# A two-layer graph attention kernel for 32 graphs: the first graph's projection taken head by head, masks of the first and last graph by transfer, W1's place used again

## The chip, the cores and the metric

The kernel runs on one core of one Trainium2 chip. The metric is the time of one execution in device microseconds (us), lower is better. Everything computed is float32. Engines are named as in the profile: PE does matrix products and PE transposes, PEld is its weight load, DVE and ACT do elementwise work, POOL issues accumulating transfers and computes one small power, SP issues all other transfers.

## The reference

For each of 32 graphs (`x` is 32 x 512 x 512, `adj` 32 x 512 x 512) the reference normalises the nodes, runs two graph attention layers and adds the result to `x`:

```python
h = relu(layernorm(x))
mask = (adj > 0) | eye(512)
h = elu(gat_layer(h, mask, W1, att_src1, att_dst1, b1, concat=True))    # H=4 heads of F=256
x = x + gat_layer(h, mask, W2, att_src2, att_dst2, b2, concat=False)    # 1 head of 512

def gat_layer(x, mask, W, a_src, a_dst, bias, concat):
    xl = (x @ W).reshape(B, N, H, F)
    asrc, adst = einsum('bnhf,hf->bnh', xl, a_src), einsum('bnhf,hf->bnh', xl, a_dst)
    e = leaky_relu(asrc[:, :, None, :] + adst[:, None, :, :], 0.2)
    attn = softmax(where(mask[..., None], e, -1e9), axis=1)
    out = einsum('bsdh,bshf->bdhf', attn, xl)
    return (out.reshape(B, N, H * F) if concat else out.mean(axis=2)) + bias
```

## The kernel before

**Work per graph.** A graph's 512 nodes are four tiles of 128 partitions. `load` brings them, `norm` computes mean and variance on DVE and the power -1/2 on POOL (one call for all four tiles), `norm_turn` scales them on ACT and turns them into `ht` (features on partitions). For the first graph the turn is made of PE transposes, for all others of a DMA transpose with two ACT passes around it. `project1` makes `xl`, four heads of 256 columns and, in two further columns of W1, the scores. `Soft.first` finds each head's softmax minimum and sum, `Soft.second` makes its weights `p` (one scalar_tensor_tensor on DVE per tile, then the mask, then an exponential on ACT), `gather1` multiplies `p` with `xl` and an ELU gives `h1`. `project2`, a second `Soft` and `gather2` do the same for layer 2, and `residual` loads `x` again with the bias added.

**Products.** Most products are taken by seven half-size products instead of eight (`sevens`, `gather1`), whose sums DVE makes ahead and whose results ACT copies (four of seven) or DVE adds (three of seven). Three are plain: the first graph's projection (`project1_first`, in the order head pair, node tile, head; all copies on ACT), and `gather1_plain` for the first graph and, through `PLAIN = 1`, for the second.

**Masks.** `masks` turns `adj` into `m`, in SBUF, keeps a copy in DRAM (`dm`) and a transposed one (`mt`). In `second` the mask is added to `p` by two accumulating transfers from `dm` on POOL's queue, except where `here` is true: three of four heads of the first graph's layer 1, and all of the last graph (four heads and layer 2). There DVE adds `m` tile by tile.

**Places.** `p` has three slots, each a whole head's weights. `w1_sb` holds W1 in seven blocks; once the last graph is projected, a part of it holds layer 2's `xl` of the last graph but one.

**Order.** `Program` records every operation with a cost and its dependences. PE's order is the order in which the program was written. The order on ACT, DVE, POOL and SP comes from a planner: rounds of list scheduling, forwards and backwards, and then 40 times a step `sooner`, which raises the rank of what TensorE waited for, over the whole program; the order with the earliest modelled end is emitted. Each engine then runs its own list in order, so an instruction that waits holds up all that stand behind it on that engine.

Of the kernel before, what the change touches and what calls it, by code (L numbers as in the profile page):

```python
# [44 lines left out]
class Program:  # L45
# [70 lines left out]
    def sooner(self, rank, start, cause):  # L116


        jobs, lost, free = self.jobs, {}, 0.0
        for j in range(len(jobs)):  # L120
            if jobs[j][0] != "PE":
                continue
            gap, free = start[j] - free, start[j] + jobs[j][1]
            d = cause[j]
            while gap > 0.05 and d is not None and start[j] - start[d] < self.SPAN:
                lost[d] = max(lost.get(d, 0.0), gap)
                d = cause[d]
        return [r - self.GAIN * lost.get(j, 0.0) for j, r in enumerate(rank)]

    SPAN, GAIN = 60.0, 2.0  # L130
# [60 lines left out]
    def order(self):  # L191
        jobs = self.jobs
        n = len(jobs)
        self.after = [[] for _ in range(n)]
        for j, job in enumerate(jobs):
            for d in job[2]:
                self.after[d].append(j)

        need, pe = [0.0] * n, None
        for j in reversed(range(n)):  # L200
            later = self.DMA_LEAD + self.DMA_TAIL + (jobs[j][4] or 0.0)
            need[j] = max(
                (
                    need[s] + jobs[s][1] + (later if jobs[j][4] is not None else self.latency(j, s))
                    for s in self.after[j]
                ),
                default=0.0,
            )
            if jobs[j][0] == "PE":
                if pe is not None:  # L210
                    need[j] = max(need[j], need[pe] + jobs[pe][1])
                pe = j
        best, self.tried = None, []

        def look(rank):
            nonlocal best
            start, done, cause = self.forwards(rank)
            end = max(start[j] + jobs[j][1] for j in range(n))
            self.tried.append(end)
            if best is None or end < best[0]:  # L220
                best = end, start, done, cause, rank
            return start, cause

        rank = need
        for _ in range(self.ROUNDS):
            back = self.backwards(rank)
            rank = [-back[j] - jobs[j][1] for j in range(n)]
            start, cause = look(rank)
            rank = [-start[j] - jobs[j][1] for j in range(n)]
        _, start, _, cause, rank = best  # L230
        for _ in range(self.REPAIRS):
            rank = self.sooner(rank, start, cause)
            start, cause = look(rank)
        _, self.start, done, _, self.late = best
        return done

    REPAIRS = 40
# [7 lines left out]
def tile_gat(  # L245
# [101 lines left out]

    prog = Program()
# [27 lines left out]
    def w1_keys(ix):  # L376
        return [("w1", ix, k) for k in range(KQ)] + [
            ("w1s", ix, k, j) for k in range(KQ) for j in range(H // 2)
        ]
# [9 lines left out]
    def weights1():  # L389
        for c in range(2):  # L390
            for r in range(2):
                for k in range(KQ):
                    row = (r * KQ + k) * P
                    ix = AT[r, c]
                    dma(
                        0.75, (), [("w1", ix, k)], w1_sb[:, ix, k, :, 2:],
                        w1[row : row + P, :].rearrange("p (j c f) -> p c j f", j=H // 2, c=2)[:, c],
                    )

    def scores1():  # L400
# [8 lines left out]
        for j in range(H // 2):  # L409
            for c in range(2):  # L410
                for a in range(2):
                    for r in range(2):
                        for k in range(KQ):
# [3 lines left out]
                                0.4, [vk + ("v", a, j), ("w1", ix, k)], [("w1s", ix, k, j), jk],  # L417
# [11 lines left out]
    def weights2():  # L429
# [11 lines left out]
        for a, v in enumerate((as2, ad2)):  # L441
            lk, bc = ls.take()
# [12 lines left out]
            ls.give(lk)  # L455
# [20 lines left out]
    def masks(b):  # L476
# [15 lines left out]
        if b < B - 1:  # L492
            MASK[b] = mk, md = mds.take()
            dma(0.45, every, [mk], md.rearrange("p t n -> p (t n)"), m.rearrange("p t n -> p (t n)"))
# [10 lines left out]
    def norm(b):  # L505
        sk, st = stats.take()
        S, A = nc.vector.BN_STATS_DIM, nc.vector.BN_AGGR_DIM
        for t, (xk, xt) in enumerate(XT[b]):
            dve(0.61, [xk], [sk + (t,)], nc.vector.bn_stats, st[:, t, :S], xt)
            dve(TINY, [sk + (t,)], [sk + (t,)], nc.vector.bn_aggr, st[:, t, S : S + A], st[:, t, :S])  # L510
        every = [sk + (t,) for t in range(NT)]
        rstd = st[:, :, S + A]
        dve(TINY, every, every, nc.vector.tensor_scalar_add, rstd, st[:, :, S + 1], EPS)
        prog.add(
            "POOL", 1.0, every, every,
            lambda: nc.gpsimd.tensor_tensor(rstd, rstd, half, op=OP.pow),
        )
        shift = st[:, :, S]
        dve(
            TINY, every, every, nc.vector.scalar_tensor_tensor,  # L520
            shift, shift, -1.0, rstd, op0=OP.mult, op1=OP.mult,
        )
        ST[b] = sk, st

    def norm_turn(b, t):
# [7 lines left out]
        if b == 0:  # L533
# [37 lines left out]

    HERE = ()
# [5 lines left out]
    class Soft:  # L578
# [96 lines left out]
        def second(self, h):  # L675
# [3 lines left out]
            pk, p = ps_.take()  # L679

            here = self.b == B - 1 or self.layer == 1 and (h in HERE or self.b == 0 and h < H - 1)
# [150 lines left out]
    def project1_first(zt):  # L832

        for j in range(H // 2):
            zk, z = zt[j]
            for t in range(NT):
                for c in range(2):
# [5 lines left out]
                           for q in (("w1", AT[r, c], k), ("w1s", AT[r, c], k, j))],  # L843
# [9 lines left out]
                    act(COPY, [bk], keys, to, bt[:, 2:W], AF.Copy, scale=-1.0)  # L853
                    dve(TINY, [bk], [zk + (0, c, t)], nc.vector.tensor_copy, z[:, 0:2, c, t], bt[:, 0:2])
                    banks.give(bk)
                yield
# [52 lines left out]
    def sums1(h, pk, p):  # L909
# [41 lines left out]
    PAIR = (  # L951
        (0, 1), (1, 1), (0, 2), (1, 2), (0, 6), (1, 6), (0, 5), (1, 5), (0, 7), (1, 7), (0, 3), (1, 3),
        (0, 4), (1, 4),
    )

    def gather1(soft, j):

        blocks, bank = {}, {}
        for i in range(2):
            blocks[i] = sums1(2 * j + i, *soft.p[2 * j + i])  # L960
        for i, n in PAIR:
            left, right, late = blocks[i]
# [4 lines left out]
            if first:  # L967
                bank[i, acc] = banks.take()
            bk, bt = bank[i, acc]
# [11 lines left out]
            g = (2 * j + i) * FPH + r  # L981
# [12 lines left out]
        for i in range(2):  # L994
            ps_.give(soft.p.pop(2 * j + i)[0])
# [51 lines left out]
    def residual(b, places=(ts_,) * NT):  # L1047

        XR[b] = []
        for d in range(NT):  # L1050
# [6 lines left out]
            dma(0.75, (), halves, xr, x[b, d * P : (d + 1) * P, :])  # L1057
# [55 lines left out]
    def gather2_plain(b, soft):  # L1113
# [17 lines left out]
        ps_.give(pk)  # L1131
# [13 lines left out]
    PLAIN = 1  # L1145
# [5 lines left out]
    norm(0)  # L1151
    for t in range(NT):
        norm_turn(0, t)
    scores1()
    masks(0)
    given = [zs.take() for _ in range(2)]
    run(project1_first(given))
# [43 lines left out]
    for i in range(B - 1):  # L1201
# [3 lines left out]
        if i < PLAIN:  # L1205
            run(gather1_plain(s, (0, 1)))
        else:
            gather1(s, 0)
        s.second(2)
        s.second(3)  # L1210
        S2[i] = second_layer(i)
        if not last:
# [11 lines left out]
        if i < PLAIN:  # L1224
            run(gather1_plain(s, (2, 3)))
        else:
            gather1(s, 1)
        if last:
            S2[i].second(0)
# [14 lines left out]
        if last:  # L1244
# [3 lines left out]
            for _ in range(4):  # L1248
# [46 lines left out]
```

## Time and profile before

| what | value |
|---|---|
| time, median of 11 runs (lowest, highest) | 2814.37 us (2806.67, 2822.99) |
| the profiled execution: time, its span | 2815.55 us, 2813.7 us |
| PE busy | 2760.0 us, 98% |
| DVE busy | 2640.7 us, 94% |
| ACT busy | 2306.9 us, 82% |
| DMA engines, mean rate | 176 GB/s |
| accumulating transfers `p<-dm` on POOL | 304, median 5.2 us from issue to landing |

The span runs from the first instruction to the last; the time of an execution has a little more around it. Busy shares are means over the whole span. PE's busy time holds stretches at a lower granted clock too, so an idle PE and a slow PE both have to be looked for. A releaser named behind an idle time is the event that came last.

### The profile page before, as it was taken

What the parts mean: (1) busy time and instruction counts of PE and PEld (TensorE: products, weight loads), DVE (VectorE), ACT (ScalarE), POOL (GpSimd) and SP (SyncE); (2) the same over time, 40 slices, a digit from 0 to 9 for tenths busy, and PEclk for the clock granted to TensorE, in tenths of its full rate; (3) what the DMA queues carried; (4) which work ended last, traced back from release to release, by engine and by line L of the source; (5) the groups of instructions that cost most, each with busy time, mean ns of one, the idle gap of its engine ahead of it and who ended that gap; (6) DMA issues with size and microseconds to landing.
All of it is one profiled execution on the core that took longest, in us unless ns stands there. A gap on an engine that the chain in (4) does not pass through costs nothing.

```text
span 2813.7 us, 41284 instructions
## 1 busy us (share of the span) xinstructions
PE 2760.0 (98%) x12456; PEld 2371.0 (84%) x12456; DVE 2640.7 (94%) x6691; ACT 2306.9 (82%) x4861; POOL 311.5 (11%) x342
## 2 busy tenths in 40 slices
PE   6999999999999999999999999999999999999988
PEld 5668888788888888888888888888888788888876
DVE  6979999899999999999999999999999899999996
ACT  6878898788888888888888888888887788888872
POOL 0011111101111011111011101011101111110100
PEclk9999999999999999999999999999999999999999
DMA  7566776667776667766676766676766767666622
GB/s 219 137 157 176 188 195 168 167 175 192 184 199 169 179 178 197 186 176 176 183 190 179 200 168 181 175 204 170 200 177 170 170 175 200 174 177 167 184 72 98
DMA packets 371600, 494.73 MB, mean 176 GB/s; under 512 B 225200, under 2 KB 229296, under 8 KB 371376
## 3 DMA queue, kind: packets, MB, share of 16 engines
q1 hardware_dynamic: 327600, 332.68, 42.3%
q0 software_dynamic: 43776, 159.40, 23.9%
q8 instruction: 100, 1.64, 0.2%
q14 instruction: 124, 1.02, 0.1%
HBM read 312.22 MB, written 50.79 MB: 129 GB/s over the span
## 4 chain that ended last, share of the span: by engine, by line
PE 48%; DVE 4%; DMA 3%; ACT 2%; issue 1%; DVEq 0%; ACTq 0%; POOLq 0%
PE mm L368 48%; DMA p<-dm 1%; DVE p L354 1%; DMA x<-adj 1%; DVE h L354 1%; ACT l L351 0%; DVE l L354 0%; DVE t L354 0%; DMA mt<-m 0%; ACT p L351 0%; DVE hs L354 0%; ACT adj L351 0%; DVE xl L354 0%; DMA t<-in_x_dram 0%; ACT ht L351 0%
## 5 line engine op out<-in xcount | busy, mean ns | idle before, releaser
L368 PE MATMUL mm<-w_sb,hs 128*128 128x257 f32 (+1 forms) x3024 | 693.9, 384 | 18.6 <-DVE hs L354 11.1
L368 PEld LDWEIGHTS mm<-w_sb,hs 128*128 128x128 f32 x3024 | 578.8, 192 | 108.4 <-DVE hs L354 12.4
L362 POOL DMA_DIRECT2D p<-dm x304 | 267.4, 889 | 2379.1 <-DVE p L354 1579.8
L351 ACT ACTIVATE l<-as,z 128x512 f32<-128x512 f32 x640 | 444.2, 721 | 93.2 <-DMA as<-das 92.5
L351 ACT ACTIVATE l<-l,low 128x512 f32<-128x512 f32 x640 | 459.0, 720 | 49.4 <-DVE low L354 47.1
L368 PE MATMUL mm<-p,xl 128*128 128x256 f32 (+1 forms) x2016 | 489.2, 391 | 9.1 <-ACT p L351 4.6
L368 PE MATMUL mm<-w_sb,ht 128*128 128x258 f32 x2112 | 483.2, 383 | 6.3 <-DVE xl L354 4.0
L351 ACT ACTIVATE p<-p,z 128x512 f32<-128x512 f32 x640 | 432.0, 719 | 49.0 <-DMA p<-dm 27.4
L368 PE MATMUL mm<-w_sb,h 128*128 128x257 f32 x2056 | 467.8, 379 | 0.0
L368 PEld LDWEIGHTS mm<-w_sb,ht 128*128 128x128 f32 x2112 | 402.4, 191 | 67.9 <-DVE xl L354 5.7
L354 DVE SCALAR_TENSOR_TENSOR p<-rr,z 128x512 f32<-128x512 f32 x640 | 453.0, 742 | 5.2 <-DMA rr<-drr 4.9
L368 PEld LDWEIGHTS mm<-p,xl 128*128 128x128 f32 x2016 | 383.2, 191 | 85.2 <-issue 20.2
L354 DVE CUSTOM_DVE_ANT_1 l<-l,mt 128x512 f32<-128x512 f32 x640 | 427.4, 681 | 19.2 <-ACT l L351 16.1
L368 PEld LDWEIGHTS mm<-w_sb,h 128*128 128x128 f32 x2056 | 389.7, 190 | 57.5 <-issue 0.5
L351 ACT ACTIVATE xl<-mm 128x258 f32<-128x258 f32 (+2 forms) x752 | 280.9, 381 | 64.2 <-PE mm L368 62.2
L351 ACT ACTIVATE h<-mm 128x256 f32<-128x256 f32 x480 | 175.3, 379 | 112.8 <-PE mm L368 109.8
L354 DVE TENSOR_TENSOR xl<-xl,mm 128x258 f32<-128x258 f32 x558 | 221.6, 416 | 35.4 <-PE mm L368 30.6
L351 ACT ACTIVATE xr<-h,b_sb 128x512 f32<-128x512 f32 x240 | 169.5, 721 | 73.3 <-DVE h L354 57.6
L368 PE MATMUL mm<-t,hs 128*128 128x256 f32 x960 | 219.3, 382 | 0.3 <-ACT h L351 0.3
L368 PEld LDWEIGHTS mm<-t,hs 128*128 128x128 f32 x960 | 183.1, 191 | 26.7 <-ACT h L351 1.0
L354 DVE TENSOR_TENSOR t<-mm,t 128x256 f32<-128x256 f32 (+1 forms) x424 | 170.6, 414 | 15.4 <-PE mm L368 14.8
L368 PE MATMUL mm<-xl,p 128*128 128x256 f32 (+1 forms) x752 | 181.0, 390 | 4.0 <-ACT p L351 4.0
(105 smaller groups left out, 3374.5 us busy)
## 6 DMA issues: line engine op xcount, KB each, us to landing
p<-dm POOLq DMA_DIRECT2D x304, 512.0 KB, 5.2
rr<-drr SPq DMA_DIRECT2D x160, 512.0 KB
x<-in_x_dram SPq DMA_DIRECT2D x129, 256.0 KB
adj<-in_adj_dram SPq DMA_DIRECT2D x128, 256.0 KB
as<-das SPq DMA_DIRECT2D x64, 512.0 KB
t<-in_x_dram SPq DMA_DIRECT2D x124, 256.0 KB
out_dram<-t SPq DMA_DIRECT2D x124, 256.0 KB
dm<-m SPq DMA_DIRECT2D x31, 512.0 KB
```

The costliest lines, as they stand in the source:

```text
L351: prog.add("ACT", cost, reads, writes, lambda: nc.scalar.activation(*a, **k))
L354: prog.add("DVE", cost, reads, writes, lambda: f(*a, **k))
L362: lambda: nc.gpsimd.dma_start(to, at, accum_op=OP.add), size,
L368: f(*a, **k)
```

## The change

The diff is cut; "..." marks what is left out. It does these things:

- W1 is loaded in 16 pieces of 128 rows by one head, head by head, where it was 8 pieces of two heads. The first graph's norm is done for each tile of 128 nodes by itself (four power calls on POOL instead of one). Its projection starts with head 0 of the tiles that are turned, between the turns, and takes heads 0 and 1 over all tiles first, then heads 2 and 3 tile by tile. The copies of every second head move from ACT to DVE.
- The second graph is turned by PE transposes too (`b < 2`), and its `gather1` is by seven products (`PLAIN = 0`).
- Masks are added by transfer everywhere but in layer 2 of the last graph. The last graph's mask is therefore kept in DRAM too.
- Heads 2 and 3 of the last graph have their `p` in two places within W1's block (`pzs`), free once that graph is projected. The last graph's four heads are gathered in one order (`SINGLY`) that runs through all of them, with `second(2)`, `second(3)` and the previous graph's layer 2 started between.
- The residual's load waits for the first tile of layer 2's projection of that graph. The vectors of layer 2's scores use a slot of `t` instead of `l`. Two instead of four products of the last graph but two's `gather2` stand ahead of the last `project2`.
- The planner's repair works through the program in stretches of 80 PE operations, tries six settings of reach and weight in each, and keeps an order when it starts the PE operation 40 behind the stretch earlier. The whole order on ACT, DVE, POOL and SP is made anew by it.

```diff
...
-    def sooner(self, rank, start, cause):
+    def sooner(self, rank, start, cause, span, gain, first, last):
...
-            while gap > 0.05 and d is not None and start[j] - start[d] < self.SPAN:
+            while gap > 0.05 and d is not None and start[j] - start[d] < span:
                 lost[d] = max(lost.get(d, 0.0), gap)
                 d = cause[d]
-        return [r - self.GAIN * lost.get(j, 0.0) for j, r in enumerate(rank)]
-
-    SPAN, GAIN = 60.0, 2.0
+        return [r - gain * lost.get(j, 0.0) for j, r in enumerate(rank)]
+
+    WAYS = tuple((span, gain) for span in (60.0, 25.0) for gain in (2.0, 0.7, 6.0))
+    STRETCH = 80
...
-        _, start, _, cause, rank = best
-        for _ in range(self.REPAIRS):
-            rank = self.sooner(rank, start, cause)
-            start, cause = look(rank)
-        _, self.start, done, _, self.late = best
+
+        _, start, done, cause, rank = best
+        n_pe = len(self.tensor)
+        for first in range(0, n_pe, self.STRETCH):
+            last = min(first + self.STRETCH, n_pe)
+            goal = self.tensor[min(last + self.STRETCH // 2, n_pe - 1)]
+            tries = deque(self.WAYS)
+            while tries:
+                new = self.sooner(rank, start, cause, *tries.popleft(), first, last)
+                if new == rank:
+                    break
+                result = self.forwards(new)
+                if result[0][goal] < start[goal] - 0.01:
+                    rank, (start, done, cause) = new, result
+                    tries = deque(self.WAYS)
+                    self.tried.append(max(start[j] + jobs[j][1] for j in range(n)))
+        self.start, self.late = start, rank
         return done
...
+    pzs = Slots(
+        "pz",
+        [
+            bass.AP(
+                tensor=w1_sb.tensor, offset=w1_sb.offset + NT * (DO + 2) + i * NT * N,
+                ap=[w1_sb.ap[0], [N, NT], [1, N]],
+            )
+            for i in range(2)
+        ],
+    )
+
+    def give_p(pk):
+        if pk[0] == "p":
+            ps_.give(pk)
+
...
-        for c in range(2):
+
+        for h in range(H):
+            j, c = divmod(h, 2)
             for r in range(2):
                 for k in range(KQ):
                     row = (r * KQ + k) * P
-                    ix = AT[r, c]
                     dma(
-                        0.75, (), [("w1", ix, k)], w1_sb[:, ix, k, :, 2:],
-                        w1[row : row + P, :].rearrange("p (j c f) -> p c j f", j=H // 2, c=2)[:, c],
+                        0.4, (), [("w1", AT[r, c], k, j)], w1_sb[:, AT[r, c], k, j, 2:],
+                        w1[row : row + P, h * FH : (h + 1) * FH],
                     )
...
-            lk, bc = ls.take()
+            lk, bc = ts_.take()
...
-        if b < B - 1:
-            MASK[b] = mk, md = mds.take()
-            dma(0.45, every, [mk], md.rearrange("p t n -> p (t n)"), m.rearrange("p t n -> p (t n)"))
+        MASK[b] = mk, md = mds.take()
+        dma(0.45, every, [mk], md.rearrange("p t n -> p (t n)"), m.rearrange("p t n -> p (t n)"))
...
+        for ts in [(t, t + 1) for t in range(NT)] if b == 0 else [(0, NT)]:
+            some = [sk + (t,) for t in range(*ts)]
+            shift, rstd = (st[:, slice(*ts), q] for q in (S, S + A))
+            dve(TINY, some, some, nc.vector.tensor_scalar_add, rstd, st[:, slice(*ts), S + 1], EPS)
+            prog.add(
+                "POOL", 1.0, some, some,
+                lambda rstd=rstd, ts=ts: nc.gpsimd.tensor_tensor(
+                    rstd, rstd, half[:, slice(*ts)], op=OP.pow
+                ),
+            )
...
-        if b == 0:
+        if b < 2:
...
-            pk, p = ps_.take()
-
-            here = self.b == B - 1 or self.layer == 1 and (h in HERE or self.b == 0 and h < H - 1)
+            pk, p = (pzs if self.layer == 1 and self.b == B - 1 and h > 1 else ps_).take()
+            if pk[0] == "pz":
+
+                for key in p_keys(pk):
+                    prog.alias(key, [k for ix in range(7) for k in w1_keys(ix)])
+
+            here = self.layer == 2 and self.b == B - 1
...
-            for t in range(NT):
-                for c in range(2):
+            for t in range(NT) if j else (None,):
+                for c, t in [(c, t) for c in range(2)] if j else [
+                    (c, t) for c in range(2) for t in range(NT)
+                ]:
...
-                    act(COPY, [bk], keys, to, bt[:, 2:W], AF.Copy, scale=-1.0)
+                    if c == 0:
+                        act(COPY, [bk], keys, to, bt[:, 2:W], AF.Copy, scale=-1.0)
+                    else:
+                        dve(ADD, [bk], keys, nc.vector.tensor_scalar_mul, to, bt[:, 2:W], -1.0)
                     dve(TINY, [bk], [zk + (0, c, t)], nc.vector.tensor_copy, z[:, 0:2, c, t], bt[:, 0:2])
                     banks.give(bk)
-                yield
+                    yield
...
-    def gather1(soft, j):
+    SINGLY = (
+        (0, 1), (0, 5), (0, 2), (0, 6), (0, 3), (1, 1), (0, 7), (1, 5), (1, 2), (0, 4), (1, 6), (1, 3),
+        (2, 1), (1, 7), (2, 5), (2, 2), (1, 4), (2, 6), (2, 3), (3, 1), (2, 7), (3, 5), (3, 2), (2, 4),
+        (3, 6), (3, 3), (3, 7), (3, 4),
+    )
+
+    def gather1(soft, order):
...
+        ahead = {h for h, n in order[:2]}
+        for h in sorted(ahead):
+            blocks[h] = sums1(h, *soft.p[h])
...
-        for i in range(2):
-            ps_.give(soft.p.pop(2 * j + i)[0])
+            if n == 4:
+                give_p(soft.p.pop(h)[0])
+                yield h
...
-            dma(0.75, (), halves, xr, x[b, d * P : (d + 1) * P, :])
+            dma(0.75, [x2_key(b, 0, 0)], halves, xr, x[b, d * P : (d + 1) * P, :])
...
-    PLAIN = 1
+    PLAIN = 0
...
+    scores1()
+    given = [zs.take() for _ in range(2)]
+    products = project1_first(given)
     for t in range(NT):
         norm_turn(0, t)
-    scores1()
+        if t > 0:
+            next(products)
     masks(0)
-    given = [zs.take() for _ in range(2)]
-    run(project1_first(given))
+    run(products)
...
-        if i < PLAIN:
-            run(gather1_plain(s, (0, 1)))
+        if last:
+            for h in gather1(s, SINGLY):
+                if h < 2:
+                    s.second(h + 2)
+                if h == 0:
+                    S2[i] = second_layer(i)
+                if h == 2:
+                    S2[i].second(0)
         else:
-            gather1(s, 0)
-        s.second(2)
-        s.second(3)
-        S2[i] = second_layer(i)
-        if not last:
+            run(gather1_plain(s, (0, 1)) if i < PLAIN else gather1(s, PAIRS_OF[0]))
+            s.second(2)
+            s.second(3)
+            S2[i] = second_layer(i)
             S2[i].second(0)
...
-            for _ in range(4):
+            for _ in range(2):
                 next(rest)
...
```

## The prediction

> **What bounds the kernel now.** I read the page's busy shares first, then PE's timeline for every idle time, then the windows for the granted clock, then the groups for prices.
>
> ```profile
> PE 2760.0 (98%) x12456; PEld 2371.0 (84%) x12456; DVE 2640.7 (94%) x6691; ACT 2306.9 (82%) x4861; POOL 311.5 (11%) x342
> ```
>
> PE is the bound: 2813.7 - 2760.0 = 53.7 us is all that it idles. PE's timeline splits this into 21.7 us before 70.1, 16.1 us from there to 2670, 12.2 us from there to 2810, and 3.7 us after the last product. DVE, at 94%, is close behind. The timeline of PE at both ends:
>
> ```profile
> 10.11 1.12 PE L368 MATMUL mm<-identf,x 128*128 128x128 f32 x4 [10.11 <-ACT x L351]
> 11.52 2.82 PE L368 MATMUL mm<-identf,x 128*128 128x128 f32 x12 [0.29 <-ACT x L351]
> 14.72 1.13 PE L368 MATMUL mm<-w_sb,ht 128*128 128x258 f32 x2 [0.38 <-issue]
> 17.55 29.41 PE L368 MATMUL mm<-w_sb,ht 128*128 128x258 f32 x134 [1.69 <-DVE xr L354]
> 49.64 3.70 PE L368 MATMUL mm<-w_sb,hs 128*128 128x258 f32 x8 [2.68 <-DVE hs L354]
> 57.33 6.75 PE L368 MATMUL mm<-w_sb,hs 128*128 128x258 f32 x16 [3.99 <-ACT xl L351]
> 63.92 3.64 PE L368 MATMUL mm<-w_sb,ht 128*128 128x258 f32 x16
> ...
> 2723.19 1.13 PE L368 MATMUL mm<-p,xl 128*128 128x256 f32 x4 [2.32 <-ACT p L351]
> 2724.59 1.31 PE L368 MATMUL mm<-p,xl 128*128 128x256 f32 x4 [0.27 <-ACT p L351]
> 2728.08 1.10 PE L368 MATMUL mm<-p,xl 128*128 128x256 f32 x4 [2.17 <-DVE h L354]
> 2729.01 5.52 PE L368 MATMUL mm<-t,hs 128*128 128x256 f32 x16
> ...
> 2794.41 15.54 PE L368 MATMUL mm<-xl,p 128*128 128x512 f32 x32 [4.00 <-ACT p L351]
> ```
>
> In brackets is the idle time and what ended it. An idle costs more than itself: sixteen matmuls take 3.64 us at 63.92 but 6.75 at 57.33. The windows say why (span, PE, PEld, DVE, ACT, POOL busy, then granted clock):
>
> ```profile
> 53.40:57.30 3.90, 0.00 (x0) 0.00 (x0) 3.15 (x11) 3.90 (x12) 0.67 (x1) 0.91 0.47 132
> 57.30:64.00 6.70, 6.67 (x17) 5.35 (x18) 2.42 (x11) 4.98 (x12) 0.34 (x1) 0.54 0.23 80
> 2672.50:2674.70 2.20, 0.07 (x1) 0.00 (x0) 1.79 (x4) 2.11 (x9) 0.00 (x0) 0.99 0.02 7
> 2674.70:2678.20 3.50, 3.48 (x9) 2.81 (x10) 2.29 (x8) 3.50 (x9) 0.86 (x1) 0.52 0.55 133
> ```
>
> After 3.9 us without a matmul the clock is 0.54 for 6.7 us, after 2.2 us still 0.52 for 3.5 us. So at the start 9.2 us of idle (2.68, 3.99, 2.52 at 70.08) bring slow clock against the usual 1.90 for eight and 3.64 for sixteen: 1.8 + 3.1 + 1.8 (16 in 5.43 at 70.08) = 6.7. That is 15.9 us in all.
>
> **The change part by part.** The profiled execution took 2815.55 us, 1.2 above the median; I save from 2815.55 and take 1.2 off at the end.
>
> *First products.* The stream now starts at 17.55; the two matmuls at 14.72 are worth 0.43. W1's four blocks of head 0 (0.52 MB), x (1.05) and the two vectors of heads 0 and 1 (0.52) are 2.1 MB. The first tile is in at 3.48; the other 1.83 MB, at the 273 GB/s of the first 15 us, are in at 10.2. The last four of head 0's eight score operations (0.35 apart) end at 11.6. By then half of the 16 transposes are done; the other 8 at 0.235 (2.82 / 12) cost 1.9. Saved: 17.55 - 0.43 - 11.6 - 1.9 = 3.6. Bounds: 0 if the vectors land at 11.1 and 13.85 as now, 5.5 if x's last two tiles land behind. Eight more issues on SP at 0.66 (2.64 / 4) are 5.3 us, ahead of `adj` and the next graph's x; ten issues precede head 0's scores, 6.6 us, inside the 10.2. Three more powers on POOL, about 1.04 each, lie between tiles. I take 3.6.
>
> *From the first to the second projection.* Now each tile of the second graph takes 1.05 + 1.36 on ACT and a DMA transpose between, and the first sum waits for them. PE transposes need a copy of 0.60 alone: 7.2 us less on ACT. Every second copy of the projection leaves ACT, 8 x 0.33 = 2.6, and costs DVE 8 x 0.34 = 2.7. The residual's adds at 33.7 to 36.6 (2.6 on DVE) and their 1 MB go behind `project2`; the loads then wait in SP's list, and what stands behind them, later loads and scores to spread, waits with them if x2 is late. Twelve mask adds, 0.60 apart, leave DVE (7.2), and six accumulating transfers come. POOL's issue takes 0.89, and landing 5.2 (4.1 to 12.1 in the trace), against 0.6 per add: hidden while PE does project1's 24 us, otherwise 5 us for each head. The 2.68 should go, since two pairs of products need no sum; the 3.99 (a copy behind exponentials on ACT) and 2.52 (an add behind others on DVE) lose most of their cause. Of 15.9 I take 10; bounds 0 and 15.9.
>
> *Transposes of the second graph.* 16 x 0.235 = 3.8 on PE if they go as at the start; half of it if that was slow as the windows at 0.5 are. I take 2.8 lost, between.
>
> *The second graph's gather.* 32 x 2 matmuls at 0.434 (13.90 / 32) are 27.8 us; 112 at 0.2172 are 24.3. Gain 3.5 on PE. DVE gets four sums of 0.34 and four of 0.60 per head and three adds of 0.34 more: 4 x 4.8 = 19 us. Cover: DVE is busy 53.0 of 71 us from 140 to 211, 18 us free. It just covers, and where the start moves forward it covers less. I take 1.5; bounds -3.5 and 3.5. The idle of 1.97 at 141.58 (ACT's p) I leave.
>
> *The last graph's heads 2 and 3.* From 2716, when heads 0 and 1 give slots back, DVE does eight score operations and eight adds in a row. PE idles 2.32 + 0.27 + 2.17 + 0.54 + 0.39 = 5.7 us, and loses 1.9 at 2729.01 (5.52 against 3.62) and 0.4 in the fours before it (1.03 usual): 8.0. All four heads' adds (16 x 0.60 = 9.6 of DVE's 67.1 in 70 us) go, and W1's place is free at 2683. Eight transfers come, 4.1 to 12.1 us each to landing, between DVE and the exponentials, with 24 us of project2 and two heads as cover. I take 6.5; bounds 0 and 8.0.
>
> *The tail.* Two products more, 8 x 0.216 = 1.7, fill the 4.00 before 2794.41. What stays, 2.3, still lowers the clock as the 2.2 above did. Saved 1.7; bounds 0 and 5.6.
>
> *At nothing.* Six small operations more in the first norm (0.16 each) lie in DVE's early idle, 8.5 of 15 us; without it they cost 1.0. One copy more of a mask to DRAM, 0.63 on SP (33.54), lies beside 24 us of products; the slots' names cost no instruction.
>
> *The planner.* All orders between change. The middle has 14.1 us of idle besides the 1.97, so at most 14 and a few of slow clock are to be won. Lost could be stalls like that at 2213.35 (5.63 idle, 2.0 slow). I take 0, bounds -8 and 8 (one such stall).
>
> Sum: 3.6 + 10 - 2.8 + 1.5 + 6.5 + 1.7 = 20.5; 2815.55 - 20.5 - 1.2 = 2793.9, say 2794.
>
> **Two rules of the skill.** The Trainium skill (TensorE: Matmul & The Clock Gate, part 1) lowers the clock only after an idle window of about 3.4 us. The 2.2 us rows above speak against it. By the rule only the 3.99 would lose clock, the 15.9 would be 12.3, the same share of it 7.7, and the sum 18.2: 2796. I go by the rows.
>
> The Trainium skill (DMA: Bandwidth & Descriptors, section Bandwidth) speaks against cutting W1: batch transfers to 1 MiB or more, about 2 us fixed for each. Eight transfers more, one behind another, would be an estimated 16 us and undo the start. The trace's 273 GB/s in pieces of 256 KB shows them overlapped.
>
> **Rivals.** *A stall of transposes, in the middle.* At 2213.35 PE waits 5.63 because ACT, in order, waits 8.2 for a DMA transpose; at 502.29 the same costs 2.83. For it: the order is all new and its model holds transfers at even speed. Against: two in 29 graphs now. At 7.6 each, three more eat the gain (2794 + 22.8 = 2817), four give 2824. It decides from 26.1 / 29 = 0.9 us per graph.
>
> *DVE bounds the start.* DVE is busy 66.6 of 70 us from 70 to 140, so an earlier PE may only wait longer before 141.58. Then the start's 12.3 is lost, 2794 + 12.3 = 2806. Against: 7.2 + 2.6 - 2.7 = 7.1 us leave DVE ahead of that, and it idles 16 in the first 50.
>
> *The transfers are late at the end.* Then 6.5 goes: 2800.
>
> *The pieces land no earlier.* W1 head by head does nothing if the queue delivers in another order: 2797.6, within the forecast.
>
> *The middle gains* one stall's worth, 7.6 or more: 2786 or less.
>
> **How the numbers follow.** The forecast (2788 to 2803, with small misses of single terms) 0.50, DVE at the start 0.15, transfers at the end 0.10, gain in the middle 0.06: faster, 0.81. Start and end both failing, 2813, is within 0.2% (5.6 us, about what a measurement of this kernel can tell): 0.09. The stalls: 0.10, slower. The range 2781 to 2811 reaches from the middle's gain with the upper bounds of two terms to both ends nearly failing; it leaves out the stalls, and a few in a hundred below and above.
>
> **What would show it.** In the changed profile: projection's stream from about 12 us; no idle over 1 us with clock near 0.5 between 40 and 75; `mm<-p` of 512 columns 64 fewer; `p<-dm` x318, `p<-p,m` x4, `x<-adj` x120; PE without a stop through the last four heads; the last idle about 2.3. Wrong: PE waiting for ACT p or DVE for long after 100 us, or idle over 5 us in the middle more than twice.

## The result and the profile after

The changed kernel takes 2795.18 us (median of 16 runs, 2788.49 to 2802.95), the kernel before beside it 2812.77 (62 runs): a ratio of 0.9943, 95% interval 0.9932 to 0.9954. By the medians it is 17.6 us faster (13 to 19 by the interval); the forecast was 2794. The profiled execution took 2794.49 us, its span is 2792.7. The busy shares on its page:

```profile
PE 2748.3 (98%) x12520; PEld 2368.6 (85%) x12520; DVE 2641.9 (95%) x6721; ACT 2303.3 (82%) x4865; POOL 325.9 (12%) x359
```

PE's idle time fell from 53.7 us to 44.4 (span less busy), and PE's busy time by 11.7. PE's timeline at the start:

```profile
11.51 2.22 PE L396 MATMUL mm<-identf,x 128*128 128x128 f32 x8 [11.51 <-ACT x L379]
13.86 2.90 PE L396 MATMUL mm<-w_sb,ht 128*128 128x258 f32 x8
...
19.51 24.53 PE L396 MATMUL mm<-w_sb,ht 128*128 128x258 f32 x112
43.87 1.91 PE L396 MATMUL mm<-identf,x 128*128 128x128 f32 x16
46.28 2.01 PE L396 MATMUL mm<-w_sb,ht 128*128 128x258 f32 x8 [0.50 <-ACT ht L379]
...
53.81 1.14 PE L396 MATMUL mm<-w_sb,hs 128*128 128x258 f32 x4 [1.83 <-ACT xl L379]
57.21 3.42 PE L396 MATMUL mm<-w_sb,hs 128*128 128x258 f32 x8 [2.26 <-ACT xl L379]
```

The first tiles are multiplied between the turns (13.86), and the second graph's sixteen PE transposes take 1.91 us at 43.87. The three idles of 2.5 to 4 us between 49 and 71 us have become 1.83 and 2.26 behind ACT's copies. After 1.83 four products take 1.14 us, nearly as usual; after 2.26 eight take 3.42 instead of 1.90. The window of those and of the transposes, with the clock after POOL's column:

```profile
43.00:46.30 3.30, 2.80 (x22) 2.40 (x20) 3.18 (x11) 3.30 (x8) 0.00 (x0) 1.00 0.22 36
57.20:60.70 3.50, 3.49 (x10) 2.85 (x11) 2.78 (x15) 2.66 (x6) 0.00 (x0) 0.58 0.81 188
```

The last two graphs in the same timeline:

```profile
2687.51 2.00 PE L396 MATMUL mm<-w_sb,hs 128*128 128x257 f32 x8 [1.55 <-ACT w_sb L379]
...
2704.86 1.13 PE L396 MATMUL mm<-w_sb,xl 128*128 128x256 f32 x4 [1.51 <-ACT w_sb L379]
...
2719.22 1.13 PE L396 MATMUL mm<-w_sb,xl 128*128 128x256 f32 x4 [1.09 <-DVE h L382]
...
2773.07 15.71 PE L396 MATMUL mm<-xl,p 128*128 128x512 f32 x32 [3.79 <-ACT p L379]
```

`w_sb` as the releaser is W1's old place. At 2704.86 it is the last graph's weights of heads 2 and 3: they wait 1.51 us there and 1.09 at 2719.22, where they waited 2.32 and 2.17. At 2687.51 it is a copy of `project2`'s result for the graph before. The last idle is 3.79 and not the 2.3 that I expected. Of the prediction's signs four fall short: the projection starts at 13.86 instead of about 12, the clock still falls before 75 us (0.58, above), the last four heads still stop, and the last idle is not 2.3. The counts came out (318 mask transfers, 4 of them into `w_sb`, and 120 turns `x<-adj`).

**Where the gain lies.** I cut each trace at the first product of `project2` of the second graph (205.6 us before) and of the last graph but one (2683.4), and at the end of the last product. "Start", "middle" and "last" are what a profiled execution won there against the profile of before, in us; "ratio" is that of all runs of a kernel to the kernel before run beside it.

| kernel | ratio [95%] | start | middle | last | sum |
|---|---|---|---|---|---|
| forecast | | 12.3 | 0 | 8.2 | 20.5 |
| after | 0.9943 [0.9932, 0.9954] | 7.1 | 9.7 | 4.4 | 21.2 |
| e1_before | one run, 2819.46 us | -0.8 | -3.1 | 0.0 | -4.0 |
| e2_plan_only | 0.9991 [0.9979, 1.0004] | 3.5 | 4.9 | -6.1 | 2.3 |
| e3_no_plan | 0.9929 [0.9917, 0.9941] | 15.1 | 7.1 | 1.3 | 23.4 |
| e4_start_only | 1.0001 [0.9986, 1.0016] | 10.2 | -4.6 | -2.9 | 2.6 |
| e5_end_only | 1.0026 [1.0009, 1.0043] | -8.1 | -2.2 | 0.0 | -10.3 |
| e6_masks_dve | 1.0043 [1.0023, 1.0062] | 7.6 | -20.9 | -2.4 | -15.6 |
| e7_plain | 1.0002 [0.9987, 1.0017] | 4.8 | -9.5 | 3.2 | -1.5 |
| e8_tail | 0.9942 [0.9927, 0.9957] | 9.8 | 8.1 | 2.0 | 19.9 |
| e9_pe_turns | 1.0097 [1.0070, 1.0124] | 12.4 | -41.1 | 5.4 | -23.3 |
| e10_dve_last | 0.9958 [0.9946, 0.9971] | 12.1 | 8.2 | -0.5 | 19.8 |
| e11_dve_first | 0.9983 [0.9969, 0.9997] | 6.9 | -1.1 | -3.7 | 2.1 |
| e12_residual | 0.9927 [0.9907, 0.9947] | 14.1 | 6.7 | -0.5 | 20.3 |

The kernel before scatters over 23 us in its 62 runs, and each stage here is one profiled execution. e1, which is the kernel before once more, differs by 3.1 in the middle; so a stage's figure is good to a few us at best. The profile of before lay 2.8 above the median of the 62 runs, so the 21.2 between the profiles are 17.6 between the medians. The sum came out as forecast, but its parts did not: the start gave 5 less, the end 4 less, and the middle, which I had put at nothing, almost 10.

### The profile page after: what moved, and what is told of

The parts are those of the page before. It is cut to its first block, busy times and chain, and to the rows that moved or that the text cites. A ratio compares the mean times of both kernels' runs of the same rounds, so it can differ in the third digit from the quotient of the medians.

```text
span 2792.7 us, 41561 instructions
## 1 busy us (share of the span) xinstructions
PE 2748.3 (98%) x12520; PEld 2368.6 (85%) x12520; DVE 2641.9 (95%) x6721; ACT 2303.3 (82%) x4865; POOL 325.9 (12%) x359
## 3 DMA queue, kind: packets, MB, share of 16 engines
q8 instruction: 100, 1.64, 0.2%
## 5 line engine op out<-in xcount | busy, mean ns | idle before, releaser
L396 PE MATMUL mm<-w_sb,hs 128*128 128x257 f32 (+2 forms) x3032 | 689.5, 381 | 11.0 <-ACT xl L379 7.2
L390 POOL DMA_DIRECT2D p<-dm x314 | 274.7, 880 | 2333.5 <-DVE p L382 1549.8
L396 PE MATMUL mm<-p,xl 128*128 128x256 f32 (+1 forms) x1984 | 466.6, 383 | 1.3 <-ACT p L379 1.3
L379 ACT ACTIVATE p<-p,z 128x512 f32<-128x512 f32 x632 | 424.5, 717 | 51.9 <-DMA p<-dm 37.8
L382 DVE SCALAR_TENSOR_TENSOR p<-rr,z 128x512 f32<-128x512 f32 x632 | 447.2, 743 | 6.9 <-DMA rr<-drr 6.6
L382 DVE CUSTOM_DVE_ANT_1 l<-l,mt 128x512 f32<-128x512 f32 x640 | 427.1, 681 | 17.6 <-ACT l L379 15.1
L396 PEld LDWEIGHTS mm<-p,xl 128*128 128x128 f32 x1984 | 376.1, 190 | 61.5 <-issue 5.4
L379 ACT ACTIVATE h<-mm 128x256 f32<-128x256 f32 x496 | 181.4, 379 | 91.4 <-PE mm L396 87.0
L379 ACT ACTIVATE xr<-h,b_sb 128x512 f32<-128x512 f32 x248 | 176.3, 721 | 81.4 <-DVE h L382 65.6
L396 PE MATMUL mm<-t,hs 128*128 128x256 f32 x992 | 225.8, 379 | 2.6 <-DVE t L382 1.9
L382 DVE SCALAR_TENSOR_TENSOR h<-h,b_sb,xr 128x512 f32<-128x512 f32 x248 | 179.2, 741 | 10.0 <-ACT xr L379 9.9
```

Of the source, the lines that this page charges most:

```text
L379: prog.add("ACT", cost, reads, writes, lambda: nc.scalar.activation(*a, **k))
L382: prog.add("DVE", cost, reads, writes, lambda: f(*a, **k))
L390: lambda: nc.gpsimd.dma_start(to, at, accum_op=OP.add), size,
L396: f(*a, **k)
```

## The experiments

**The middle: chance or order?** e1 is the kernel before, unchanged.

> The kernel before once more, unchanged, for a second profile. Theory A (the change made three pieces: about 6 us in the first 110 us, about 10 us from 2670 on, and 5 us in the middle that are two chance stalls of the first profile at 502 and 2213): the idle of PE between 160 and 2670 us is again 15 to 25 us with its slow clock, but the long stall is at another place or missing; the losses before 160 us (34 us) and after 2670 us (20 us) return at the same places within 2 us. Rival B (the stalls belong to the old order): 2.8 and 5.6 us of idle at 502 and 2213 again.

```profile
2216.72 8.00 PE L368 MATMUL mm<-w_sb,hs 128*128 128x258 f32 x24 [5.71 <-DVE hs L354]
```

The stall that stood at 2213.35 is there again with 5.71 instead of 5.63 us, and so are those at 502 (1.98 at 504.1, instead of 2.83) and 2674 (2.15 at 2678.6, as before). By this one repeat they belong to the order, not to chance; one of 1.87 at 2254.5 is new. How the large one arises, in the profile of before: the issues on SP's queue and POOL, then the waiting instruction on ACT.

```profile
2196.14 4.20 SPq L556 DMA_TRANSPOSE x<-adj  x2
```
```profile
2196.90 0.86 POOL L362 DMA_DIRECT2D p<-dm  x1 [13.39 <-PE mm L368]
2198.83 0.86 POOL L362 DMA_DIRECT2D p<-dm  x1 [1.07 <-PE mm L368]
```
```profile
2211.23 1.34 ACT L351 ACTIVATE ht<-x 128x1024 uint16<-128x1024 uint16 x1 [8.25 <-DMA x<-adj]
```

Two turns of the next graph (`x<-adj`) and two accumulating transfers are issued within 3 us. The second transfer lands after 12.1 us instead of the usual 5.2, and the turn reaches ACT only at 2211.23. ACT, in order, stands for 8.25 us; DVE's sums wait for `ht`, and PE for the sums. Such a meeting alone is not enough. In the 13 traces other than e9, two turns and two accumulating transfers were issued within 3.1 us of one another 20 times, and the second transfer took over 10 us in four of them (before, e1, e4, e8).

**The planner alone, and all but the planner.** e2 is the kernel before with the new planner, e3 the kernel after with the old one. The diffs from here on are cut to the lines that tell the runs apart; a comment names the run.

```diff
+    def sooner(self, rank, start, cause):          # e3: as before
+    SPAN, GAIN = 60.0, 2.0
+    REPAIRS = 40
-    WAYS = tuple((span, gain) for span in (60.0, 25.0) for gain in (2.0, 0.7, 6.0))
-    STRETCH = 80
```

> The kernel before with the new planner alone. Theory A: the planner only reorders what bounds nothing most of the time, so 0 to 6 us faster, ratio 0.998 to 1.000, the start's first product at 17 us and the idle before the last graph's heads 2 and 3 still there. Rival B (the planner makes the gain, the other edits follow): 12 us or more faster, ratio 0.9957 or less.

> The kernel after with the planner of before. Theory A: 11 to 17 us faster than before, ratio 0.994 to 0.996. Rival B: under 6 us faster, ratio 0.998 or more.

e2 can't be told from the kernel before, and e3 has at least as much of the gain as the changed kernel (their intervals overlap). The new planner brings nothing that shows. It won 4.9 in e2's middle and lost 6.1 at its end; with the old one the start is worth 15.1 instead of 7.1.

**Start and end alone.** e4 is the kernel before with W1 by heads, the norm by tiles, the first projection's new order, its copies on DVE and the second graph's PE transposes. e5 is the kernel before with the last graph's mask in DRAM, `pzs`, `SINGLY` and two products of `gather2` ahead; the first graph's masks stay on DVE. Neither has the seven products for the second graph (both keep `PLAIN = 1`), the first graph's masks by transfer or the residual's wait.

```diff
+                        0.4, (), [("w1", AT[r, c], k, j)], w1_sb[:, AT[r, c], k, j, 2:],   # e4
+        if b < 2:                                                                          # e4
+            here = self.layer == 2 and self.b == B - 1 or self.layer == 1 and self.b == 0 and h < H - 1   # e5
```

> The kernel before with the start's edits alone: W1 by heads, norm by tiles, projection between the turns with half its copies on DVE, second graph turned by PE. Masks, the second graph's plain gather, the end and the planner as before. Theory A: the first product of layer 2 starts 5 to 9 us earlier than before's 113.3 us, since the three mask adds stay on DVE and no transfer has to land before the exponentials; whole kernel 3 to 9 us faster, ratio 0.997 to 0.999. Rival C (DVE bounds the start, and only masks by transfer free it): the first product of layer 2 not earlier than 111 us, ratio 0.999 to 1.001.

> The kernel before with the end's edits alone (last graph's masks by transfer, heads 2 and 3 in W1's place, the four heads in one order, two products ahead), planner and start as before. Theory A2 (start and end each give 6 to 12 us of their own; what is left over is decided by how often, in the middle, two DMA transposes meet two accumulating transfers in the new order): the stretch from the last graph's first layer-2 score to the end as in the kernel after, so the idle times of 2.2 to 2.3 us before heads 2 and 3 are gone, 6 to 10 us less lost after 2670 us; the whole -10 us plus or minus 8 by the middle. Rival D (the end gains only since the masks leave DVE over the whole order, and the places do nothing): under 3 us less lost after 2670.

e4 starts the first `project2` 10.4 us earlier than before and keeps 10.2 to the second. Then new stalls eat it, the largest the same picture as in the kernel before:

```profile
1862.58 1.34 ACT L351 ACTIVATE ht<-x 128x1024 uint16<-128x1024 uint16 x1 [9.04 <-DMA x<-adj]
```
```profile
1864.70 8.21 PE L368 MATMUL mm<-w_sb,hs 128*128 128x258 f32 x24 [5.91 <-DVE hs L354]
```

A transfer issued there at 1849.66 took 14.7 us to land. e5 is slower: with an order in which the first graph's gather waited for ACT's `p` (4.81, 4.27 and 6.12 us) the first `project2` starts 11.3 us late, and nothing is won at the end. Neither part does what its edits do in the whole; but together they are not the whole, so the rest is not priced by this pair.

**The masks.** All on e3. e6 has DVE add the masks of the first and of the last graph's layer 1, e11 the first's alone, e10 the last's alone.

```diff
-            here = self.layer == 2 and self.b == B - 1
+            here = self.b == B - 1 or self.layer == 1 and self.b == 0 and h < H - 1                      # e6
+            here = self.layer == 2 and self.b == B - 1 or self.layer == 1 and self.b == 0 and h < H - 1  # e11
+            here = self.b == B - 1                                                                       # e10
```

> The kernel after with the planner of before, and with the first graph's three heads and the last graph's four masked by DVE adds as before. Theory A2: the start as good as without this edit within 3 us (the adds are shorter than a transfer's landing), the end 2 to 5 us worse, the whole 0 to 6 us slower than the kernel after with the old planner, ratio to before 0.993 to 0.996. Rival D: the end loses all its gain, 8 us or more, ratio 0.996 or more.

> The changed kernel under the old planner, with the first graph's masks of three heads added by DVE again. By the forecast's reason (7.2 us of adds leave DVE) the first project2 starts some 5 us later than e3_no_plan's 105.1 and the second later than its 190.5. The rival, from e6_masks_dve, where the first project2 started at 104.2 with these adds on DVE: the masks of the first graph cost nothing before project2, and the gain there comes from the rest of the start. Then 105 within 1.5 us. On the whole 0.993 to 0.996; above 0.998 if a middle with stalls as in e6_masks_dve comes with it.

> The changed kernel under the old planner, with the last graph's masks in layer 1 added by DVE again; W1's places and the order SINGLY stay. It separates the two halves of the forecast's term of 6.5 at the end. If the adds were what held the products, the loss after the second last project2 grows from e3_no_plan's 14.2 us to about 18 to 20, with PE waiting for ACT's p after 2700. If the places and the order alone did it, it stays within 1.5 us of 14.2. The rival on the whole: every new order shifts the middle by some 10 us whatever the edit; then the ratio leaves 0.993 to 0.996 for a reason that lies before 2640 us.

The first graph's masks don't move the first `project2` (104.2 and 104.1 us, 105.1 in e3), so the rival was right there. They move the second. The windows from the first `project2` to the second (span, then PE, PEld, DVE, ACT and POOL busy, the clock) of e3, e6 and e11:

```profile
105.10:190.50 85.40, 85.40 (x394) 74.09 (x393) 83.42 (x201) 73.46 (x157) 8.66 (x10) 1.00 0.62 162
```
```profile
104.20:197.90 93.70, 87.29 (x393) 75.39 (x392) 90.04 (x226) 81.34 (x175) 10.54 (x11) 0.96 0.65 162
```
```profile
104.10:198.70 94.60, 88.37 (x394) 75.73 (x393) 90.80 (x225) 79.12 (x170) 10.54 (x11) 0.96 0.62 161
```

The products need 85 us, and in e3 PE runs through them. The twelve adds themselves lie before 91 us; what they push back leaves DVE 90 to 91 us of work in this stretch, and PE idles 6.2 to 6.3 us and loses clock. In e6 all of it is one wait for DVE:

```profile
114.16 3.78 PE L384 MATMUL mm<-w_sb,h 128*128 128x257 f32 x8 [6.28 <-DVE h L370]
```

In e11 it is 1.66 us for DVE's `h` and 4.28 for ACT's `p`. So this is the rival "DVE bounds the start", avoided by the transfers; in e11 it is DVE's directly only in part.

In e10 the last stage as a whole gains 1.8 less than in e3 (-0.5 against 1.3), less than the expected 4 to 6. But between the last two `project2`, where the adds lie, e10 takes 60.7 us against 57.6 in e3, and the kernel before 61.1. The windows of that stretch in before, the changed kernel, e3 and e10 (columns as above):

```profile
2683.40:2744.50 61.10, 55.40 (x241) 45.54 (x240) 60.85 (x133) 42.58 (x92) 0.88 (x1) 0.97 0.22 65
2666.70:2721.90 55.20, 51.04 (x233) 43.61 (x232) 55.20 (x132) 45.41 (x100) 8.20 (x10) 1.00 0.66 181
2661.20:2718.80 57.60, 53.34 (x233) 44.70 (x233) 55.45 (x132) 46.39 (x99) 7.76 (x9) 0.97 0.61 168
2663.10:2723.80 60.70, 53.22 (x233) 42.86 (x233) 60.68 (x138) 43.98 (x96) 0.86 (x1) 1.00 0.28 88
```

With the adds DVE is busy all through, and the places and the order alone win 0.4 us. It is busy all through in the changed kernel too, but with 5.6 us less to do. In the six profiles whose last graph is masked on DVE (before, e1, e2, e4, e6, e10) it has 60.3 to 61.1 us of work there, in the eight others 54.5 to 59.4. So it is the transfers that take work off DVE here; an order can still lose the time again (e5 takes 60.3 us, e11 62.4). Behind this part e10 is 1.4 us shorter than e3, which its edit does not explain. By the medians e10 is 9.8 us slower than e3, while the spans of the two profiles differ by 3.6: e10's profiled execution was the fastest of its twelve.

**The second graph's gather.** e7 is e3 with `PLAIN = 1`.

```diff
-    PLAIN = 0
+    PLAIN = 1
```

> The changed kernel under the old planner, but the second graph's gather plain again (PLAIN = 1). It prices the gather term. By the forecast (term 1.5, bounds -3.5 to 3.5) the stretch from the first to the second project2, 85.4 us in e3_no_plan, is 1.5 longer, at most 3.5 if the 19 us of DVE's sums were fully covered; it is shorter if DVE was the bound there. The rival: the stretch is decided by what the order puts beside it and moves by more than 3.5 either way. The whole, within 4 us of e3_no_plan (ratio 0.991 to 0.995) if only the term counts; 0.997 and above if the middle's stalls come anew.

From the first to the second `project2` it takes 95.1 us against 85.4: 9.7, far outside 1.5 to 3.5. The products alone are some 3.5 of it (the prediction's 27.8 against 24.3); the rest is this idle and the slow clock behind it (its PE timeline):

```profile
168.56 8.15 PE L384 MATMUL mm<-p,xl 128*128 128x512 f32 x12 [3.83 <-ACT p L367]
```

Twelve plain products take 5.42 us elsewhere. Plain products need not bring such an idle: e5, with plain products too, idles 0.47 us in this stretch and takes 89.1 us, 3.7 more than e3. Nor do seven products always take it away: the changed kernel idles 4.2 us there. So of e7's 9.7 some 3.5 are the products', and the rest is its own order's. The middle of e7 is 16.6 us worse than e3's besides.

**Turning without transfers.** e9 is e3 with every graph turned by PE; `x<-adj` is gone.

```diff
-        if b < 2:
+        if True:
```

> The kernel after with the planner of before, and with all graphs turned by PE transposes, so that no DMA transpose of the nodes is left to meet the accumulating transfers. Theory A2 (collisions make the stalls of the middle): PE does 30 x 16 transposes more at 0.109 us, 52 us, and the longest idle of PE between 160 and 2670 us is under 1.5 us; idle there 5 us or less in all; 40 to 50 us slower than without this edit, so 18 to 32 us slower than before. Rival E (the stalls come from the other loads or from chance, not from transposes): idle times of 2 to 6 us in the middle as before, 10 us or more in all.

Some 30 graphs by 16 transposes of 0.109 us are 52 us on PE, and the span grows by 46.7. PE's idle from 215 to 2640 us falls from 10.3 in e3 to 7.6, its longest to 1.58 (expected: 5 in all, none over 1.5). The waits of ACT for transfers: in e3

```profile
ACT l L367 <- DMA as<-das: 83.2, 35, 5.3
...
ACT p L367 <- DMA p<-dm: 36.5, 27, 4.0
...
ACT ht L367 <- DMA x<-adj: 18.2, 6, 7.3
```

and in e9

```profile
ACT l L367 <- DMA as<-das: 177.7, 52, 6.8
...
ACT p L367 <- DMA p<-dm: 61.1, 44, 3.1
```

(us in total, times, longest). None of the long stalls is left without the turns, though ACT waits longer for transfers as a whole. That does not show the turns as the cause by itself: ACT also has 183 us less work, and PE some 50 us more, so everything else has more time in each graph.

**The tail.** e8 is e3 without products of `gather2` ahead of the last `project2`, and with the last residual loaded early into places of its own; e12 has the second edit alone.

```diff
-            for _ in range(2):
+            for _ in range(0):                                     # e8
-            dma(0.75, [x2_key(b, 0, 0)], halves, xr,
+            dma(0.75, [x2_key(b, 0, 0)] if b < B - 1 else (), halves, xr,   # e8, e12
-    residual(B - 1)
+    residual(B - 1, (xrs,) * NT)                                   # e8, e12
```

> The kernel after with the planner of before, and three more edits at the end: no product of the last graph but two's gather ahead of the last project2 (two more lie behind it), the last residual in the slots of xr, and its load waiting for nothing. Theory A2: the idle before the last sixteen products of 512 columns falls from 3.8 us to 0 to 2, with the slow clock behind it; 2 to 4 us faster than the same without these edits, ratio to before 0.991 to 0.993, plus or minus 0.002 by the middle. Rival: the last chain (scores, spread, score sums, second spread, exponential) grows by what is put beside it, as it did in the kernel after (26.8 us against 25.5), and the idle stays over 3 us.

> The changed kernel under the old planner, with the last graph's residual loaded into places of its own and without the wait for layer 2's projection; two products stay ahead of the last project2. If the loads and stores on SP in front of the last scores' transfer made the last idle 3.8 us, it falls to about 2.3, as in e8_tail, and 1.5 us are won at the end: 0.9924 where the rest is as in e3_no_plan. The rival: the order made anew takes it back elsewhere (the start or the middle move by more than 1.5 us), and the ratio is 0.992 to 0.996 without a difference that can be measured.

The last idle falls to 2.33 in e8 and 3.19 in e12, from 3.80; but it is 3.19 in e6, e7, e10 and e11 too, whose residual is that of e3, so e12's fall is not shown to be its edit's. From the last `project2` to the first plain product it is 25.7 us in e12 against 26.4 in e3 and 26.6 in the changed kernel. Between the last two `project2` e12 takes 59.9 us, 2.4 more than e3, with this stall some 60 us earlier (PE's timeline of e12; e3 has 2.32 in its place):

```profile
2710.24 3.68 PE L384 MATMUL mm<-w_sb,xl 128*128 128x256 f32 x8 [3.23 <-ACT w_sb L367]
...
2772.75 16.91 PE L384 MATMUL mm<-xl,p 128*128 128x512 f32 x32 [3.19 <-ACT p L367]
```

The rival was right: no gain that can be measured. e12 and e3 have the lowest ratios of all, 0.9927 and 0.9929, but their intervals overlap that of the changed kernel; no version is shown to beat it.

## Why the prediction was right, and where it was not

The time was right and the direction was argued from the right places; the agreement to 1 us is luck, since three stages missed by 4 to 10 us in ways that cancel, and the profile that the sum started from lay 2.8 us above the later median.

- **First products: 3.6, measured 1.2.** The first projection ends at 43.87 instead of 45.05. With the same instructions in the old planner's order it is 2.9 (e3) and 3.2 (e12). The pieces of W1 did not hold the stream, and the estimate of 16 us for eight more of them did not come true. I had costed the order at nothing: here the first turn came at 11.51, 1.4 us later than before. But one profile does not resolve this term: in the four without the start's edits (before, e1, e2, e5) the first projection ends at 43.7 to 48.9 us, and before and e1, the same kernel, differ by 3.8; in the ten with them it ends at 41.8 to 44.6.
- **Transposes of the second graph: 2.8 lost, measured 1.9.** They run at a clock of 1.00 directly behind the projection, 0.109 us each. The start's 0.235 is about twice that, as at half clock, but the window from 0 to 15 us shows a clock of 1.00, so what made it slow stays open. The Trainium skill (TensorE: Matmul & The Clock Gate, part 4) says that full clock doesn't engage for transposes; here sixteen in a row, behind products, kept it. Whether transposes alone would reach it isn't shown.
- **First to second projection: 10, measured 7.0.** From the second projection's first product to the first `project2` it took 68.2 us and takes 61.2 (61.3 in e3). PE's idle there fell only from 9.2 to 6.0: the copies on ACT, which I let go with their cause, still end the 1.83 and 2.26. The transfers were not needed for this term: in e4, where DVE adds these masks, the same stretch took 56.0 us. That a gap of 2.2 us can cost clock was right: 1.5 us lost in the eight products behind 2.26. By the rule of 3.4 us (the Trainium skill, TensorE: Matmul & The Clock Gate, part 1) nothing would have been lost there; the row decides. It is not so each time: in e5 24 products behind 2.31 us took 5.49, against the usual 5.38.
- **The second graph's gather: 1.5, measured 1.3** (92.3 to 91.0 us), but 7.0 in e3's order and 9.7 between e7 and e3. In the changed kernel PE's busy time in the stretch fell by 3.6 us (90.33 to 86.72) and its idle time rose from 2.0 to 4.2, 1.90 of it behind one of DVE's sums (`t`): DVE's cover fell just short, as the 1.5 had allowed. In e3's order it held: DVE is busy 83.4 of 85.4 us and PE doesn't wait. The difference of 5.7 between the two is the order's.
- **Heads 2 and 3: 6.5, measured 5.9** between the last two `project2`, up to 1.7 of it the two products that the tail's term moved out of it. The mechanism was right in that the adds held DVE: its work there fell from 60.85 to 55.20 us. With the places and the order alone (e10) the stretch is 0.4 us shorter than before.
- **Tail: 1.7, measured -1.4.** The two products do fill the wait, but the wait grew: from the last `project2` to the first plain product it is 26.6 us instead of 25.4, because `rr<-drr` is issued 2.33 us after `drr<-rr` instead of 1.64, behind the residual's and the output's transfers on SP, and what it brings is used 5.6 us after its issue instead of 4.7. Counted with the two products that this part has more, it is 0.3 us shorter. I had taken the chain behind `project2` as fixed.
- **The planner: 0, right** by e2 and e3.
- **The middle: 0, measured 9.7**, beyond the bound of 8. It has none of the stalls at 502, 2213 and 2674; its longest idle is 1.69. The bound took one such stall as the limit, where more than one could go at once.

**The rivals.** The stall behind a late turn is real and repeats with an order (before and e1; e4). e4 lost its gain to one of 5.91 us and smaller ones, e6 to three of 3.2 to 3.5, close to "three more eat the gain"; but only the first of e6's is behind a turn (ACT waits 6.95 us for `x<-adj`), the other two follow waits for `p<-dm` (4.23 and 2.37). The chance of 0.10 was too low for a change whose order is made anew: of the five changed orders that lack a part of the start's work (e4, e5, e6, e7, e11), four are no faster than before. DVE bounding the start is what e6 shows, and e11 in part, as the price of not doing the masks by transfer.

**What the middle pays for.** In the 13 traces other than e9 I took each stretch from one `project2` to the next, from the third to the thirtieth, 351 in all. Some 225 of them take within 0.5 us of the time of their products. Sorted by when the third of the four turns in the stretch is issued, counted from the stretch's start, the 288 below 25 us lose 0.4 to 0.5 us each, 33 between 25 and 26 lose 1.6, and 30 at 26 or later lose 4.4, and all of these over 1 us. (In the stall of before it is 26.8.) So these 63 stretches hold some 60% of the middle's loss, and in them a late turn can meet the accumulating transfers of the next heads. But a stall early in a stretch would delay the turn and lengthen the stretch alike, so which causes which isn't shown. What makes the turn late differs; in the two that I followed (before at 2169, e7 at 2096) it was an ACT pass ahead of the turn, in e7 late behind an accumulating transfer that took 12.5 us. This is a regularity of the traces; only e9 bears on it, and e9 changes the load of PE and ACT too.

**What stays open.** The five kernels that have all of the start's edits (after, e3, e8, e10, e12) gain 6.7 to 9.7 in the middle, the seven others with transposing transfers at most 4.9. How work before 200 us reaches the graphs a millisecond later isn't shown: the list order of every later graph is made from the same ranks, which is an argument and no measurement. A rival is the residual's wait for layer 2's projection, an edit that, like the planner, touches every graph of the middle. No run takes out this edit alone: e4 and e5 lack it and lose 4.6 and 2.2, and e6, e7 and e11 have it and lose too, so it is not enough by itself. So the largest single part of the gain stays without a shown cause.

## What to carry to other kernels

Where an order is made anew for each edit, price the edit by its stage and expect the rest to move by as much again: run the edit with the old order, and parts of it alone, before a gain is put down to it. An engine that is 94% busy over the kernel can be the bound in the stretch where work is added or taken away, so take the sum of its work over that stretch (here DVE's between the last two `project2`). An idle time whose cause is thought gone should be asked what else it waits for: of those at the start, two stayed behind copies on ACT.

## What was not expected of the hardware

Accumulating transfers that are issued beside a transposing one sometimes land very late. In the two stalls followed above they took 12.1 and 14.7 us, against medians of 5.2 and 5.4 in these runs, and ACT waited 8.25 and 9.04 us for the turn. In the 13 traces other than e9, 48 of 1007 transfers with a turn issued within 3 us of them took over 10 us, and 5 of 3009 without one.

The clock can fall after idle times of little over 2 us: eight products took 3.42 us after 2.26 (usual 1.90), but 2.00 after 1.55. The length alone does not decide it: 24 products lost almost nothing after 2.31 us in e5.
